# A four-layer gated transformer: layer 0's attention, norms and routing run as a pipeline over groups of 512 tokens, with reciprocals from ScalarE's Ln and Exp and a Newton step

## The chip, the cores and the metric

The kernel runs on one core of a Trainium2 chip. The metric is the device time of one execution in microseconds. A core has five engines with queues of their own, each of which works its instructions off in order: TensorE (PE: matmuls, with a second row for its weight loads), VectorE (DVE), ScalarE (ACT), GpSimd (POOL) and SyncE (SP, which here only issues DMAs). ACT and POOL issue DMAs too. Every wait between engines is a semaphore.

## The reference, cut to what matters

There are four layers; each adds a gated cross-attention and a gated mixture of experts to the residual x of 2 x 1024 tokens of 256 values. The change is in layer 0 alone:

```python
x = x + tanh(g_xattn[0]) * L0_xattn(layernorm(x), ctx, Wq, bq, ..., Wo, bo, gamma, beta)
x = x + tanh(g_ffn[0])   * L0_ffn(layernorm(x), Wr, br, W1, b1, W2, b2)
```

As the kernel computes it, layer 0's attention is linear. With h = layernorm(x), q = elu(h Wq + bq) + 1 and k the same of the context; kv = k^T v and ksum = the sum of k over the context's 64 tokens, per batch. The attention's values are (q kv) / (q ksum + 1e-6), with the division element by element per channel; these go through Wo, plus bo, plus h; a layer norm with gamma and beta follows, and the result times the gate is added to x.

Layer 0's experts: h = layernorm(x), softmax over 8 experts of h Wr + br, each token goes to its best expert. Tokens are sorted by expert into tiles of 128 slots (at most 23 tiles); each tile goes through that expert's W1, ReLU, W2, and is added back into x with its weight.

All values are float32.

## The kernel before, in words

The 2048 tokens lie in SBUF as `xs`, 16 tiles of 128 tokens by 256 values; four tiles are a group of 512 tokens. The kernel's stages follow one another: `xattn0` (layer 0's attention), `moe0` (its experts), `middle` (layer 1 and layer 2's attention), `moe_capacity` for layer 2, `heads_xattn` (layer 3's attention), `moe_capacity` for layer 3. A scheduler lays the instructions of each engine in an order when the program is built, from the order in the source and from estimated costs; instructions of neighbouring stages are mixed where the data allow. Tiles come from pools with a fixed number of buffers; a tile waits until the buffer's last reader is through.

`xattn0` in the order of its source:

- Four loads of weights, then k, v, kv and ksum of the context (L236, L239), copied out of PSUM by `evac`, which takes DVE and ACT in turn (L147, L145).
- `normed` (all four groups first): `norm_group` calls `stats` (bn_stats L154 and bn_aggr L155 per tile; then 1/sqrt by an integer first guess, L160 and L161, and three Newton rounds of three DVE instructions on four columns, L165 to L168), writes h with one DVE instruction per tile (L178), transposes it on PE (L186) and copies the transposes to hT, one half by DVE, one by ACT.
- For each group and each of the two halves of the channels (128 channels by 512 tokens; the prediction calls this a chunk): hT times Wq on PE; DVE takes min(.+bq, 0) into `qlo` (L258), ACT its Exp (L259) and the Relu of the positive part (L261), POOL adds both into q (L262); DVE computes the denominator `rden` (L263) and its reciprocal (L267). Then q times kv on PE and the product with `rden` on DVE (L272, `att`).
- For each tile: att times Wo on PE, plus bo on DVE (L277), plus h on POOL (L278), then `stats` again, two DVE instructions for the normed value and gamma (L282, L286), and two POOL additions into xs, of beta and of y (L287, L288).

`moe0` then takes the norms of all four groups again, stores h and x in two DRAM tables `hd` and `xd` (SP, L719), and calls `route`: router logits of all 16 tiles into one PSUM tile, softmax and choice by small DVE steps on 128x128 values (L628 to L650), ranks by cumulative matmuls with `upper` and `ones` (L661, L663). Sixteen more matmuls give the counts per expert (L813, `cnt`). From the counts come the expert of each of the 23 tiles (`ex_i`, `wrow`, L820 to L853) and each token's slot; `invert` turns the slots into a table of token indices by one-hot matmuls (`ohl`, `ohh`, L691 to L704; `idx`, L710). Only then does the loop over the 23 tiles run: POOL gathers W1, W2 and the biases by `wrow` (L858, into the six buffers of `wpool`) and the tokens by `idx` (L739), PE computes, POOL scatters the result into `xd` (L772).

## Time and profile before

| What | Value |
|---|---|
| runs shown | 2466.1, 2443.22, 2464.13 us; median 2464.13 us |
| profiled execution, its own time | 2454.52 us |
| its span in the trace | 2452.7 us, mean granted PE clock 0.922 |
| PE busy | 2199.9 us (90% of the span) |
| DVE busy | 1255.2 us (51%) |
| ACT busy | 757.9 us (31%) |
| POOL busy | 1072.5 us (44%) |
| DMA | 235.07 MB, mean 96 GB/s |

How to read the profile: a group's row gives line, engine, operation, output<-inputs, shapes and count, then busy us and mean ns of one, then the idle time of the engine just before and who ended it. A timeline row gives start and duration in us, engine, line, operation, and in brackets the idle time before it. A row of a stretch gives for each engine the busy us and in brackets the number of instructions, then PE's granted clock (1.00 is full), the DMA share and GB/s. L12 is line 12 of the kernel.

### The profile page before, as it was taken

The numbers are of one execution on the slowest core, as the hardware profiler recorded it, in microseconds if no ns is written. First come the engines' busy times: TensorE is split into PE (matmuls) and PEld (weight loads), VectorE is DVE, ScalarE is ACT, GpSimd is POOL, SyncE is SP. The second block draws the span as 40 slices with busy tenths as digits, with TensorE's granted clock in tenths as the row PEclk, the third lists the DMA queues.
The fourth block names the chain that finished last, engine by engine and source line by source line (L and its number), as shares of the span: only waits on it lengthen the run. The fifth ranks groups of instructions, "written<-read, shape, count | busy, mean of one in ns | idle before, by whom it ended". The sixth has DMA issues, their size and how long they took to land.

```text
span 2452.7 us, 27852 instructions
## 1 busy us (share of the span) xinstructions
PE 2199.9 (90%) x10132; PEld 1787.2 (73%) x10132; DVE 1255.2 (51%) x2742; ACT 757.9 (31%) x1431; POOL 1072.5 (44%) x1229
## 2 busy tenths in 40 slices
PE   5558887899999999999999999999968996986997
PEld 3357775588888778887788887888856774565775
DVE  7851003676566765655865656566551116663111
ACT  1003332353333533334433334333311221330221
POOL 3316664236666346665366664666303320000331
PEclk9758998899999989999999999999958998875998
DMA  3018887012222123222132222222413543010442
GB/s 97 26 59 270 275 248 241 1 52 86 86 86 87 50 63 91 89 88 73 48 95 88 88 91 78 86 86 86 141 66 86 139 112 92 18 58 22 116 116 51
DMA packets 97544, 235.07 MB, mean 96 GB/s; under 512 B 13184, under 2 KB 41088, under 8 KB 86976
## 3 DMA queue, kind: packets, MB, share of 16 engines
q1 hardware_dynamic: 70880, 159.14, 20.3%
q0 software_dynamic: 21456, 68.92, 10.3%
q10 hardware_dynamic: 5072, 5.23, 0.6%
q8 instruction: 81, 1.33, 0.2%
q14 instruction: 55, 0.45, 0.1%
HBM read 211.10 MB, written 24.25 MB: 96 GB/s over the span
## 4 chain that ended last, share of the span: by engine, by line
PE 74%; DVE 11%; DMA 5%; POOL 3%; issue 2%; ACT 2%; POOLq 0%; ACTq 0%; DVEq 0%; SPq 0%
PE ps_b L1036 12%; PE ps_m L198 10%; PE ps_e L1036 8%; PE ps_a L1036 8%; PE ps_y L765 8%; PE ps_b L1081 6%; PE ps_a L1081 4%; PE ps_e L1081 4%; PE ps_y L198 3%; PE ps_y L434 2%; DMA xg<-hd,idx 2%; PE ps_m L704 1%; PE ps_tr L186 1%; DMA xd_L<-y_ff,idx 1%; PE ps_y L386 1%
## 5 line engine op out<-in xcount | busy, mean ns | idle before, releaser
L1036 PE MATMUL ps_b<-xsum,w 128*128 128x256 f32 x1536 | 388.2, 381 | 2.3 <-DVE c L1062 2.2
L1036 PEld LDWEIGHTS ps_b<-xsum,w 128*128 128x128 f32 x1536 | 289.7, 190 | 47.6 <-issue 4.6
L943 POOL TENSOR_TENSOR w<-w 128x256 f32<-128x256 f32 x192 | 140.8, 734 | 404.0 <-DMA w<-in_L_Wu_dram 174.6
L1036 PE MATMUL ps_a<-hT,w 128*128 128x256 f32 x1024 | 270.0, 384 | 0.7 <-DVE hT L147 0.6
L198 PE MATMUL ps_m<-xT,w 128*128 128x128 f32 (+2 forms) x1248 | 253.8, 364 | 11.8 <-DVE xT L147 11.7
L765 PE MATMUL ps_y<-w,mid 128*128 128x256 f32 (+1 forms) x1136 | 252.8, 379 | 0.0
L198 PEld LDWEIGHTS ps_m<-xT,w 128*128 128x128 f32 x1248 | 188.5, 200 | 71.9 <-DVE xT L147 19.3
L765 PEld LDWEIGHTS ps_y<-w,mid 128*128 128x128 f32 (+1 forms) x1136 | 206.6, 184 | 38.9 <-issue 2.7
L988 ACT COPY u<-ps_b 128x512 f32<-128x512 f32 (+1 forms) x192 | 98.9, 515 | 411.0 <-PE ps_b L1081 264.0
L1036 PEld LDWEIGHTS ps_a<-hT,w 128*128 128x128 f32 x1024 | 194.2, 193 | 31.2 <-issue 3.2
L772 POOL DMA_INDIRECT xd_L<-y_ff,idx x48 | 74.9, 1561 | 232.4 <-DVE y_ff L771 135.8
L770 DVE TENSOR_TENSOR y_ff<-ps_y,b 128x256 f32<-128x256 f32 (+1 forms) x48 | 20.3, 423 | 298.0 <-PE ps_y L765 298.0
L944 POOL TENSOR_TENSOR w<-w 128x256 f32<-128x256 f32 x192 | 166.9, 869 | 0.0
L946 POOL TENSOR_TENSOR w<-w 128x256 f32<-128x256 f32 x192 | 158.9, 827 | 14.7
L945 POOL TENSOR_TENSOR w<-w 128x256 f32<-128x256 f32 x192 | 164.8, 859 | 0.0
L1036 PE MATMUL ps_e<-xsum,w 128*128 128x256 f32 x512 | 134.4, 383 | 0.0
L1036 PE MATMUL ps_e<-hT,w 128*128 128x256 f32 x512 | 134.1, 382 | 0.0
L1081 PE MATMUL ps_b<-t,w 128*128 128x256 f32 x512 | 132.8, 384 | 0.0
L1081 PE MATMUL ps_a<-b,w 128*128 128x256 f32 x512 | 132.0, 379 | 0.0
L970 ACT COPY ps_b<-ps_a 128x512 f32<-128x512 f32 (+1 forms) x192 | 96.5, 502 | 109.5 <-DVE b L1066 63.5
L1098 POOL TENSOR_TENSOR m<-m,accT 128x256 f32<-128x256 f32 x60 | 71.7, 1195 | 124.1 <-ACT m L976 110.4
L145 ACT COPY xT<-ps_tr 128x128 f32<-128x128 f32 (+2 forms) x39 | 13.4, 344 | 355.7 <-PE ps_tr L748 289.4
(306 smaller groups left out, 3928.5 us busy)
## 6 DMA issues: line engine op xcount, KB each, us to landing
w<-in_L_Wg_dram SPq DMA_DIRECT2D x64, 512.0 KB, 4.1
w<-in_L_Wu_dram SPq DMA_DIRECT2D x64, 512.0 KB, 4.1
w<-in_L_Wd_dram SPq DMA_DIRECT2D x64, 512.0 KB, 3.7
w<-in_L_W_dram SPq DMA_DIRECT2D x32, 1024.0 KB, 4.9
xd_L<-xs SPq DMA_DIRECT2D x8, 512.0 KB, 2.9
hd_L<-h SPq DMA_DIRECT2D x8, 512.0 KB, 3.0
xs<-in_x_dram SPq DMA_DIRECT2D x4, 512.0 KB, 10.5
xd<-xs SPq DMA_DIRECT2D x4, 512.0 KB, 2.9
```

The costliest lines, as they stand in the source:

```text
L198: T.matmul(ps, lhsT=lhs(c), rhs=rhs(c), start=(c == 0), stop=(c == n - 1))
L765: T.matmul(ps[:w, :], lhsT=mid[:, f, at : at + w], rhs=w2[:, f, :], start=(f == 0), stop=(f == NF - 1),)
L772: G.indirect_dma_start(out=xd[:, :], out_offset=bass.IndirectOffsetOnAxis(ap=idx[:w, j0 + s : j0 + s + 1], axis=0), in_=y[:w, :], in_offse ...
L943: G.tensor_add(s[0], a21, a22)
L944: G.tensor_sub(s[1], s[0], a11)
L945: G.tensor_sub(s[2], a11, a21)
L946: G.tensor_sub(s[3], a12, s[1])
L970: A.copy(self.b, self.pa)
L988: A.copy(u2, self.b)
L1036: T.matmul(ps[:, q * 256 : (q + 1) * 256], lhsT=lhs[kind][:, q, :], rhs=xr[kind], start=(first and q == 0), stop=True, skip_group_check=True,)
L1081: T.matmul(ps, lhsT=wd[kind][:, q, :], rhs=m["rhs"][kind][:, q * 256 : (q + 1) * 256], start=(clear and q == 0), stop=True, skip_group_che ...
L1098: G.tensor_add(sb, sb, acc[:, i, j])
```

## The change

`xattn0` and the routing of `moe0` become one pipeline over the four groups, with three parts: `begin` (norm, q, the first guess of the reciprocal), `finish` (kv, Wo, second norm, addition into xs) and `onward` (the experts' norm and routing of this group). In the source order begin runs one group ahead of finish and two ahead of onward. The routing works per group (`choose`), with a running count `before` (`cnt`) carried from group to group.

The reciprocal 1/d becomes a guess r = Exp(-Ln(d)) on ACT and one Newton step, r (2 - d r). The sign is turned: DVE computes att = (d r - 2) * (ps * r), the product with Wo then has the wrong sign, and it is subtracted from h + bo. 1/sqrt in these norms becomes Exp(-0.5 Ln(v)) on ACT and one Newton round. An explicit load puts the table with both Ln and Exp on ACT after the gates' Tanh. h and both hT copies of these norms are made by ACT. h + bo and x + beta are made once per group by POOL, on 128x1024 values.

```diff
-    A.activation(gates, gates, AF.Tanh)
+    tanh = A.activation(gates, gates, AF.Tanh)
+    with tc.issue_after(tanh.ins):
+        A.preload_act_table_set("natural_log_exp_and_others")
...
+        if by_log:                                   # in stats
+            y = small.tile([P, TG], F32, name="y0")
+            A.activation(y, ve, AF.Ln)
+            A.activation(y, y, AF.Exp, scale=-0.5)
...
-        for i in range(3):
+        for i in range(1 if by_log else 3):
...
+            off = small.tile([P, TG], F32, name="off")   # in norm_group
+            V.scalar_tensor_tensor(off, mv[:, :, 0], -1.0, rstd, ALU.mult, ALU.mult)
...
+                A.activation(
+                    h[:, t, :], xg[:, t, :], AF.Identity,
+                    bias=off[:, t : t + 1], scale=rstd[:, t : t + 1],
+                )
...
-            evac(c, hT[:, c, :], ps)
+            evac(1 if by_act else c, hT[:, c, :], ps)
...
+            def begin(g):
+                h, hT = norm_group(g, pt, hpool, hTp, by_act=True)
+                w = wpool.tile([P, 2048], F32, name="w")
+                q, inv = (w[:, i : i + 1024].rearrange("p (c n) -> p c n", c=NC) for i in (0, 1024))
...
                     V.tensor_scalar(lo, ps, bq, 0.0, ALU.add, ALU.min)
                     A.activation(lo, lo, AF.Exp)
-                    hi = two.tile([P, GW], F32, name="qhi")
-                    A.activation(hi, ps, AF.Relu, bias=bq)
-                    G.tensor_add(q[:, c, :], lo, hi)
-                    V.tensor_scalar(
-                        rden[:, c, :], q[:, c, :], ksum[:, b, c : c + 1], 1e-6,
-                        ALU.mult, ALU.add,
-                    )
-                    V.reciprocal(rden[:, c, :], rden[:, c, :])
+                    A.activation(q[:, c, :], ps, AF.Relu, bias=bq)
+                    G.tensor_add(q[:, c, :], q[:, c, :], lo)
+                    ks = ksum[:, b, c : c + 1]
+                    A.activation(inv[:, c, :], q[:, c, :], AF.Ln, bias=tiny, scale=ks)
+                    A.activation(inv[:, c, :], inv[:, c, :], AF.Exp, scale=-1.0)
+                    den = two.tile([P, GW], F32, name="den", bufs=6)
+                    A.activation(den, q[:, c, :], AF.Identity, bias=tiny, scale=ks)
+                    V.tensor_mul(den, den, inv[:, c, :])
+                    dens.append(den)
+                G.tensor_add(h, h, rows[:, R_BO0, :].unsqueeze(1).to_broadcast([P, TG, D]))
+                xg = residual(g)
+                G.tensor_add(xg, xg, bet.unsqueeze(1).to_broadcast([P, TG, D]))
...
+            def finish(g):
...
-                    V.tensor_mul(att[:, c, :], ps, rden[:, c, :])
+                    V.tensor_mul(att[:, c, :], ps, inv[:, c, :])
+                    V.scalar_tensor_tensor(
+                        att[:, c, :], dens[c], 2.0, att[:, c, :], ALU.subtract, ALU.mult
+                    )
...
-                    V.tensor_add(y[:, t, :], ps, rows[:, R_BO0, :])
-                    G.tensor_add(y[:, t, :], y[:, t, :], hs[g][:, t, :])
-                mv, rstd = stats(y, TG)
+                    V.tensor_sub(y[:, t, :], h[:, t, :], ps)
+                mv, rstd = stats(y, TG, True)
...
-                    V.tensor_mul(y[:, t, :], y[:, t, :], gam)
-                    G.tensor_add(xt, xt, bet)
-                    G.tensor_add(xt, xt, y[:, t, :])
+                    V.scalar_tensor_tensor(
+                        y[:, t, :], y[:, t, :], mv[:, t, 0:1], gam, ALU.subtract, ALU.mult
+                    )
+                    V.scalar_tensor_tensor(
+                        xt, y[:, t, :], rstd[:, t : t + 1], xt, ALU.mult, ALU.add
+                    )
+            def onward(g):
+                h, hT = norm_group(g, pt, hp2, by_act=True)
+                routed(g, h, hT, pr)
+            begun = {}
+            begin(0)
+            for i in range(NG + 2):
+                if i + 1 < NG:
+                    begin(i + 1)
+                if 0 <= i - 1 < NG:
+                    finish(i - 1)
+                if 0 <= i - 2:
+                    onward(i - 2)
...
+    def choose(psp, rp, g, hT, which, bias, top, before):    # as route, for one group
...
+        T.matmul(ps[:, :W], lhsT=upper, rhs=flat, start=True, stop=False)
+        for k in range(1, TG):
+            T.matmul(
+                ps[:, k * E : W], lhsT=ones, rhs=flat[:, : (TG - k) * E],
+                start=False, stop=(k == TG - 1),
+            )
+        pc = psp.tile([P, 512], F32, name="ps_m")
+        for t in range(TG):
+            T.matmul(
+                pc[:, :E], lhsT=ones, rhs=both[:, t, :], start=(t == 0), stop=(t == TG - 1)
+            )
...
+        V.tensor_add(before, before, pc[:, :E])
...
+            def routed(g, h, hT, psp):
+                ts = slice(g * TG, (g + 1) * TG)
+                for d, src in ((hd, h), (xd, residual(g))):
+                    nc.sync.dma_start(
+                        d[g * GW : (g + 1) * GW, :].rearrange("(t p) d -> p t d", p=P), src
+                    )
+                ((p1, o, _, rk),) = choose(psp, rp, g, hT, 0, e_bias[:, 0, :], 1, cnt)
...
+                V.tensor_tensor(
+                    ohl[:, ts], ramp.unsqueeze(1).to_broadcast([P, TG, P]), bc(lo, P),
+                    ALU.is_equal,
+                )
```

The low half of a token's slot, its one-hot `ohl` and its number are thus made per group; after the last group `moe0` adds the tile of its expert, makes `ohh` in two halves of 8 tiles and runs the same 16 matmuls to `idx`. The tile loop is unchanged in the source. In the built order of the changed kernel the order of the tile loop on POOL differs at its start (two weight gathers ahead of the first gather of tokens, where it was three), and the instruction lists of the engines agree from the end of layer 0's experts on.

## The prediction

> **What bounds the kernel now.** I read the page first, then a table of stretches, the groups of VectorE (DVE) instructions, and last the timeline around the hand-over to the experts.
>
> ```profile
> span 2452.7 us, 27852 instructions
> ...
> PE   5558887899999999999999999999968996986997
> DVE  7851003676566765655865656566551116663111
> ```
>
> A slice is 61 us. TensorE (PE) is full from slice 8 on; the change touches the first three slices only. So what counts is the time at which the experts of layer 0 can start.
>
> ```profile
> 30.00:40.00 10.00, 7.49 (x15) 2.99 (x14) 10.00 (x24) 3.00 (x5) 2.84 (x4) 0.83 0.00 0
> 100.00:110.00 10.00, 2.11 (x3) 1.08 (x4) 9.65 (x21) 1.21 (x2) 3.54 (x4) 0.50 0.15 52
> 140.00:160.00 20.00, 17.37 (x78) 16.07 (x78) 8.20 (x35) 1.76 (x3) 0.00 (x0) 0.50 0.24 79
> 160.00:180.00 20.00, 10.72 (x64) 10.62 (x64) 9.15 (x36) 0.31 (x1) 3.16 (x2) 0.59 0.03 7
> 240.00:260.00 20.00, 17.26 (x110) 15.03 (x109) 1.96 (x6) 6.82 (x19) 14.27 (x14) 1.00 0.89 279
> ```
>
> Columns: stretch, length, then PE, weight load, DVE, ScalarE (ACT), GpSimd (POOL) busy, PE clock, DMA share, GB/s. From 30 to 135 us DVE is the bound (10.00 and 9.65 of 10). From 135 to 178 us nothing is: layer norm, router and ranks are one chain of short steps, with PE at half clock. From 178 us on the experts pull weights at a DMA share near 0.9.
>
> ```profile
> L267 DVE RECIPROCAL rden<-rden 128x512 f32<-128x512 f32 x8 | 26.7, 3340 | 0.0
> L178 DVE TENSOR_SCALAR h<-xs,mv,rstd 128x256 f32<-128x256 f32 x28 | 12.7, 514 | 0.0
> L282 DVE TENSOR_SCALAR y_sb<-y_sb,mv,rstd 128x256 f32<-128x256 f32 x16 | 9.0, 606 | 0.0
> L263 DVE TENSOR_SCALAR rden<-q_sb,ksum 128x512 f32<-128x512 f32 x8 | 4.3, 531 | 0.0
> ```
>
> Eight reciprocals of 3.34 us take a quarter of DVE's 105 us.
>
> ```profile
> 33.60 1.26 POOL L262 TENSOR_TENSOR q_sb<-qlo,qhi 128x512 f32<-128x512 f32 x1
> 33.65 1.24 DVE L161 TENSOR_SCALAR yi<-yi 128x4 int32<-128x4 int32 x1
> ...
> 173.78 0.17 DVE L818 COPY cnt<-ps_m 128x8 f32<-128x8 f32 x1 [4.60 <-PE ps_m L813]
> ...
> 176.55 0.19 DVE L853 CAST wrow<-ex 128x23 int32<-128x23 f32 x1
> ...
> 178.03 2.68 POOL L858 DMA_INDIRECT w<-in_L_W_dram,wrow  x1 [0.30 <-DVE ohh L695]
> ...
> 188.41 0.24 DVE L710 TENSOR_SCALAR idx<-ps_m,spare 128x23 int32<-128x23 f32 x1 [7.16 <-PE ps_m L704]
> ```
>
> wrow at 176.7 us opens the weight stream, idx at 188.7 the gather of tokens; the first expert matmul comes at 192.9. I count the gain in wrow.
>
> **The reciprocals.** DVE loses 26.7 + 4.3 us and gains, per chunk (one group, one half of the channels), den times inv and (den - 2) times att: two 128x512 passes of about 0.60 (nearest row: att L272, 0.68 out of PSUM), 9.6 in all. ACT gains Ln, Identity and Exp per chunk, 24 passes. Rows: Exp L259 0.63, Relu with a bias column L261 0.67; so some 0.65, 15.6 us. **A rule against it**: the Trainium skill, "ScalarE: Activation LUTs", What it computes, says to leave reciprocals to VectorE; What ACT_TABLE_LOAD costs prices an ACTIVATE at 186 ns + 0.833 ns an element + 93 ns per column operand. Ln and Identity have two such columns, 0.80 us each by the page, Exp 0.61: 17.7 us. The rows show only 0.04 us for one column, so I take 15.6; the page's 2 us more would be on the path only in part. DVE is the bound and ACT idles, so by the rows the rule fails here: 31.0 off DVE against 9.6 back. A table load costs 1.28 in the trace (gates); the change adds one, in the wait for the gates at the start, free; if Ln and Exp switched tables the price would be up to 16 x 1.28 = 20 us, but the built instruction list holds only the one load between gates and the middle.
>
> **The norms.** h (L178) and both hT copies go to ACT (32 x about 0.45, 8 x 0.59), two of three Newton rounds and the yi steps go (about 20 us of the DVE groups L160 to L168, most of it port waits), L282 and L286 (9.0 + 6.0) become two fused 128x256 passes (32 x 0.41 = 13). DVE's busy time falls by some 50 us, ACT's rises by 40. Neither is the gain, since the order of the queues decides.
>
> **The longer POOL adds.** xs + bet and h + bo become eight 128x1024 adds: between 2.35 us (line through 0.77 for 256 and 1.30 for 512 columns) and 3.0 (four times 0.75); I take 2.7. The two lines from 33.6 us show a DVE instruction of four columns held for the whole POOL add: 1.24 us. The Trainium skill, "SBUF — State Buffer", Who interferes with whom, says the same of every DVE instruction with two SBUF inputs against a GpSimd one that reads SBUF: the later one waits for all of it. So the wait per meeting rises from 1.3 to 2.7 us. By the row alone (tensor_scalar) the norm of group 2 would meet none, and start 3 us sooner; by the rule, its q and rstd steps meet xs + bet and h + bo. I count 3 us there.
>
> **The path, from the built order.**
> 1. First qlo at 30.2 us before, about 28 after (the first 20 us are input DMA, both hT copies are on ACT, the 3 us lock is in it); then ACT still has the rest of group 2's h: Exp at 29.7.
> 2. Groups 0 to 2 are six chunks. Each next Exp of lo stands on ACT behind this chunk's last Exp: 0.54 (Exp, start to start in the trace) + 0.67 + POOL add 1.30 + Ln 0.70 + 2 x 0.55 = 4.3. Queued behind the Ln that waits for POOL are the two passes and hT copies, and PE waits for those. 6 x 4.3 = 26, and 2 more for POOL's xs + bet of group 2 in front: 57.
> 3. Group 3's statistics stand in DVE's queue behind y of group 0, whose rest stands behind the last den product of group 2. From there to rstd of group 3 are some 22 instructions, 8 us: 65. h, transposes, hT, wq: 5. Two chunks at 4.3, and POOL's two 2.7 us adds in front, 1.5: 80.
> 4. From den(3,1) to rstd of onward(2) DVE has 174 instructions: 12 y subtractions, 24 fused passes at 0.34 (start to start), 28 statistics pairs at 0.40, seven 128x512 at 0.60, 74 small of routing, rstd and copies at about 0.08 and two ohl of 0.6: 4.1 + 8.2 + 11.1 + 4.2 + 6.1 + 1.2 = 35. Waits for wo (before: 1.0, 1.06 and 1.31 us in three groups), for the router and Ln/Exp: between 2 and 18 (PE at full clock, or at half); I take 6, as before's clock was 0.8 to 0.9 where PE had this much to do. 121.
> 5. Tail, two groups in turn: h, transposes, hT, router at half clock 7.5 + 0.7 (before: 8.5); routing of 128x32 steps at 0.2: 3; cumulative matmuls 16 x 0.165 = 2.6; router of group 3 3.6; routing 3; 2.6; ranks and cnt 0.8; then cmp to wrow, before 2.8, now 5.6, because ohl and six ohh passes stand ahead of wrow: 29. **wrow 150, against 176.7: 27 us sooner.**
>
> The long count over 16 tiles (62 records, 4.92 + 5.35) leaves the path; the four short ones, 16 records each, lie beside other work except in the tail. ohl off the path saves 2 us of the 11.9 from wrow to idx, and ohh ahead of wrow 2 more; idx comes 7 us after wrow. POOL now issues two weight loads before the gather instead of three; 2 MB need about 8 us at 270 GB/s, as long as that wait, so nothing is lost. If DMA sets the experts' pace the end moves by 27, if the token loop does by 31: **29**. On SP the stores of xd and hd are now interleaved per group (hd(g) behind xd(g+1)); the last hd is stored in the tail's 29 us, 3 us long: hidden.
>
> The profiled execution took 2454.5 us (span 2452.7): 2454.5 - 29 = 2425.5. Its own time lies between the runs shown (2443 to 2466, median 2464); against that median the result would read 1.6% lower, against itself 1.2%.
>
> **Rivals.**
> - *The bubbles close* (0.22). If DVE worked without a wait from 29 us on, its queue is 24 + 35 us and wrow comes at 29 + 59 + 29 = 117: 60 sooner. For: DVE has had no idle time in the stage. Against: step 2 makes it wait for ACT and POOL. Half of the bubbles filled: 45 us, **2410**.
> - *PE at half clock sets the pace* (0.20). In step 4 a group has 16 wo records at 0.43, 8 transposes 1.95, router 3.6: 12.4 us of PE at half clock against 11.7 of DVE, in turn for each tile; waits become 18 instead of 6: gain 17, **2438**. For: clock 0.50 from 100 us. Against: PE idles less than before.
> - *The port lock* (0.08). POOL's adds sum to 8 x 2.7 + 8 x 1.3 = 32 us, all before 80 us, where DVE has some 28 instructions with two SBUF inputs. If each POOL add holds such a one that others wait for, up to 32 us come on top of the path: 29 - 32 = -3, **2458**. It decides from 29 us of such waits. Against: ACT paces that stage, and DVE has slack there.
>
> The forecast has 0.50, with its own range of a gain of 18 to 38 us. With run noise of about 10 us the range is 2402 to 2450: it takes in the closed bubbles at 45 and the half clock. One per cent, 24.6 us, is about what a measurement of this kernel can tell from no change: faster 0.36 (of the forecast) + 0.22 = 0.58; same 0.14 + 0.20 + 0.02 = 0.36; slower 0.06.
>
> **What would show it.** The weight gathers start near 150 us; the ACT timeline shows 4.3 us a chunk up to 57 us; DVE idles 20 us or more between 30 and 80 and hardly after 80; POOL adds of 2.4 to 3 us with DVE instructions of that length beside them; the expert stage keeps 9.4 us a tile. Wrong: if wrow comes before 135 or after 165, or if it comes at 150 and the kernel's end does not move with it.

## The result and the profile after

The changed kernel took 2439.65 us (median of 20 runs, 2431.99 to 2454.38) beside 2459.43 us for the kernel before (20 runs). The ratio over all these runs is 0.9943, 95% interval 0.9929 to 0.9957; it is not the quotient of the two medians, which lie 19.8 us apart. Of 2459.43 us it makes 14.0 us, between 10.6 and 17.5, where the forecast was 29. In the profiled executions the spans are 2452.7 and 2435.4 us. A gain under 1% was the "same" of the prediction, to which it gave 0.36.

The page of the changed kernel, its span and the busy tenths of TensorE (PE) and VectorE (DVE) in slices of 61 us:

```profile
span 2435.4 us, 27851 instructions
...
PE   5668887899999999999999999999968996886997
DVE  5631113675565766655855656566551116663111
```

DVE's first two digits were 7 and 8; they are 5 and 6. PE's row is full from slice 8 on, as before. So work did leave DVE, and the question is what the end gained from it. The same five stretches as before (length, then PE, weight load, DVE, ScalarE (ACT), GpSimd (POOL) busy, PE clock, DMA share, GB/s):

```profile
30.00:40.00 10.00, 8.44 (x21) 4.59 (x22) 1.76 (x4) 6.60 (x13) 6.67 (x4) 0.69 0.00 1
100.00:110.00 10.00, 6.02 (x37) 4.89 (x35) 8.30 (x41) 2.45 (x7) 0.00 (x0) 0.84 0.15 52
140.00:160.00 20.00, 14.84 (x65) 13.65 (x64) 7.13 (x42) 2.07 (x6) 0.00 (x0) 0.50 0.08 27
160.00:180.00 20.00, 11.00 (x51) 10.45 (x52) 5.70 (x30) 1.28 (x4) 10.21 (x11) 0.51 0.57 210
240.00:260.00 20.00, 17.12 (x101) 15.01 (x100) 2.04 (x6) 6.42 (x18) 12.77 (x13) 0.91 0.83 252
```

In the first row DVE fell from 10.00 busy of 10 to 1.76, and no other engine is full either: ACT 6.60, POOL 6.67, PE 8.44 at a clock of 0.69. A bound was taken away and a chain of hand-overs stands in its place. In the last row, the expert stage, PE's clock is 0.91 (1.00 before) and the weights come at 252 GB/s (279).

From 28 us to wrow, the index list that opens the weights' stream, the first row below is the kernel before, the second the changed one:

```profile
28.00:176.60 148.60, 93.53 (x310) 61.91 (x308) 116.65 (x333) 14.47 (x25) 42.10 (x52) 0.70 0.08 29
28.00:165.00 137.00, 90.84 (x319) 61.22 (x320) 79.19 (x319) 50.14 (x102) 22.58 (x14) 0.72 0.09 31
```

DVE lost 37.5 us of work and gained 25.9 us of idle time (148.60 - 116.65 = 32.0; 137.00 - 79.19 = 57.8). The stretch became 11.6 us shorter: what is left of 37.5 when 25.9 are waited away. The groups of DVE instructions of that stretch name the waits (busy us, mean ns, then the idle time ahead and who ended it):

```profile
L281 DVE TENSOR_SCALAR qlo<-ps_m,cols 128x512 f32<-128x512 f32 x8 | 6.0, 749 | 16.9 <-PE ps_m L217 16.9
L292 DVE TENSOR_TENSOR den<-den,w 128x512 f32<-128x512 f32 x8 | 5.6, 698 | 7.5 <-ACT w L289 7.5
...
L727 DVE TENSOR_TENSOR r_cum<-ps_m,cnt 128x32 f32<-128x32 f32 x4 | 0.8, 192 | 5.7 <-PE ps_m L717 5.7
L684 DVE TENSOR_TENSOR r_pr<-ps_m,e_bias 128x32 f32<-128x32 f32 x4 | 0.8, 192 | 9.9 <-PE ps_m L217 9.9
```

The largest, 16.9 us, is for the first product of a group (qlo). The timeline shows what it waits for:

```profile
26.01 2.27 DVE L176 SCALAR_TENSOR_TENSOR q<-q,ve 128x4 f32<-128x4 f32 x1
...
30.95 0.61 ACT L282 ACTIVATE qlo<-qlo 128x512 f32<-128x512 f32 x1
31.12 2.35 POOL L297 TENSOR_TENSOR xs<-xs,bet 128x1024 f32<-128x1024 f32 x1 [2.86 <-ACT h L192]
...
34.72 0.81 ACT L288 ACTIVATE w<-w,tiny,ksum 128x512 f32<-128x512 f32 x1 [0.96 <-POOL w L284]
...
36.67 0.61 ACT L282 ACTIVATE qlo<-qlo 128x512 f32<-128x512 f32 x1
...
69.34 0.16 DVE L189 SCALAR_TENSOR_TENSOR off<-mv,rstd 128x4 f32<-128x4 f32 x1
69.53 2.08 ACT L192 ACTIVATE h<-xs,off,rstd 128x256 f32<-128x256 f32 x4 [0.82 <-DVE off L189]
72.81 5.85 PE L217 MATMUL ps_m<-hT,wq 128*128 128x512 f32 x8 [0.46 <-ACT hT L150]
76.70 0.75 DVE L281 TENSOR_SCALAR qlo<-ps_m,cols 128x512 f32<-128x512 f32 x1 [7.21 <-PE ps_m L217]
...
164.98 0.18 DVE L1029 CAST wrow<-ex 128x23 int32<-128x23 f32 x1
```

From 69.34 to 76.70 us DVE, ACT and PE hand one group's norm, transposes and first product to each other, each idle while another works, and DVE stands 7.21 us. wrow comes at 165.0 instead of 176.6.

The other half of the result lies in the expert stage. The last of its 23 scatter-adds, in the kernel before and in the changed one:

```profile
407.87 1.58 POOL L772 DMA_INDIRECT xd<-y_ff,idx  x1 [7.67 <-DVE w L340]
```

```profile
404.03 1.58 POOL L899 DMA_INDIRECT xd<-y_ff,idx  x1 [7.78 <-DVE w L392]
```

Of the 11.6 us only 3.8 are left here. From the first scatter to the last a tile took 9.25 us before (204.4 to 407.9, 22 steps) and 9.88 after (186.6 to 404.0). So two things are to be explained: 11.6 us at wrow instead of 27, and 7.8 us lost behind it.

The spans of the two profiles differ by 17.3 us, though, and only 3.8 of these had been gained at the last scatter. The rest lies behind it, where both kernels run the same instructions (stretch and columns as above, the kernel before first):

```profile
407.87:2452.70 2044.83, 1902.07 (x8594) 1547.10 (x8592) 1092.73 (x2233) 666.54 (x1194) 876.33 (x1017) 0.94 0.27 81
404.03:2435.40 2031.37, 1889.25 (x8594) 1537.84 (x8592) 1090.33 (x2233) 665.25 (x1194) 876.92 (x1017) 0.94 0.27 82
```

The same 8594 matmul records kept PE busy 12.8 us longer in the kernel before; with one digit more its clock is 0.936 there and 0.944 in the changed kernel. In the profiles of the 18 other kernels of this document this part took 2023.3 to 2045.4 us, 2034.5 on average, and less time the higher the clock (0.950 with 2023.3 us, 0.937 with 2045.4). So the causes are read from the times up to the last scatter, and the end gives the size only.

### The profile page after: what moved, and what is told of

Read it like the earlier page. It is cut to its first block, busy times and chain, and to the rows that moved or that the text cites. A ratio compares the mean times of both kernels' runs of the same rounds, so it can differ in the third digit from the quotient of the medians.

```text
span 2435.4 us, 27851 instructions
## 1 busy us (share of the span) xinstructions
PE 2189.6 (90%) x10132; PEld 1782.7 (73%) x10132; DVE 1210.5 (50%) x2695; ACT 797.9 (33%) x1523; POOL 1054.2 (43%) x1189
## 3 DMA queue, kind: packets, MB, share of 16 engines
q0 software_dynamic: 21456, 68.92, 10.3%
## 4 chain that ended last, share of the span: by engine, by line
PE 76%; DVE 10%; DMA 4%; POOL 2%; ACT 2%; issue 2%; POOLq 0%; DVEq 0%; ACTq 0%; SPq 0%
PE ps_b L1210 13%; PE ps_m L217 11%; PE ps_e L1210 9%; PE ps_a L1210 9%; PE ps_y L892 8%; PE ps_b L1255 6%; PE ps_a L1255 4%; PE ps_e L1255 4%; PE ps_y L486 2%; PE ps_y L217 2%; DMA xg<-hd,idx 1%; DVE st L159 1%; PE ps_tr L205 1%; DMA xd_L<-y_ff,idx 1%; PE ps_y L438 1%
## 5 line engine op out<-in xcount | busy, mean ns | idle before, releaser
L217 PE MATMUL ps_m<-xT,w 128*128 128x128 f32 (+2 forms) x1248 | 260.6, 372 | 16.4 <-DVE xT L152 16.0
L217 PEld LDWEIGHTS ps_m<-xT,w 128*128 128x128 f32 x1248 | 195.6, 208 | 76.1 <-DVE xT L152 23.2
```

What stands on the lines that cost most here:

```text
L217: T.matmul(ps, lhsT=lhs(c), rhs=rhs(c), start=(c == 0), stop=(c == n - 1))
```

## The experiments

The times at which the milestones came, each in the one profiled execution, and the measured ratios. "To last" is the time from wrow to the last scatter; "order" is that of POOL's queue in the expert stage (a: as in the changed kernel, b: as in the kernel before, t: token rows ahead). Each ratio is taken against runs of the kernel before in the same round (medians from 2451 to 2457 us for e1 to e17), so it is not the quotient with 2459.43.

| Kernel | order | wrow | last scatter | to last | median us | ratio to before, 95% |
|---|---|---|---|---|---|---|
| before | b | 176.6 | 407.9 | 231.3 | 2459.43 | 1 |
| changed | a | 165.0 | 404.0 | 239.1 | 2439.65 | 0.9943 (0.9929 to 0.9957) |
| e1 scatter late | own | 166.4 | 404.0 | 237.7 | 2441.68 | 0.9940 (0.9917 to 0.9962) |
| e2 idle matmuls | a | 164.7 | 404.3 | 239.6 | 2443.18 | 0.9941 (0.9919 to 0.9964) |
| e3 tokens ahead | t | 165.3 | 400.0 | 234.7 | 2441.51 | 0.9941 (0.9919 to 0.9962) |
| e4 before, tokens ahead | t | 174.5 | 415.4 | 240.9 | 2458.41 | 1.0010 (0.9994 to 1.0025) |
| e5 e3 + Relu on DVE | t | 166.0 | 379.0 | 213.1 | 2417.74 | 0.9864 (0.9840 to 0.9887) |
| e6 half the weights | a, smaller loads | 165.4 | 399.6 | 234.2 | 2433.93 | 0.9937 (0.9913 to 0.9960) |
| e7 pipeline alone | a | 173.9 | 405.7 | 231.8 | 2444.18 | 0.9968 (0.9955 to 0.9981) |
| e8 reciprocals alone | b | 156.9 | 390.5 | 233.6 | 2424.51 | 0.9883 (0.9855 to 0.9910) |
| e9 changed, order b | b | 166.5 | 397.2 | 230.6 | 2435.07 | 0.9922 (0.9890 to 0.9954) |
| e10 norms on DVE | a | 177.4 | 415.4 | 238.0 | 2452.79 | 0.9996 (0.9972 to 1.0019) |
| e11 den on DVE | a | 165.9 | 404.7 | 238.8 | 2437.95 | 0.9936 (0.9918 to 0.9955) |
| e12 e8 + t + Relu on DVE | t | 155.7 | 390.4 | 234.8 | 2427.93 | 0.9889 (0.9853 to 0.9924) |
| e13 attention's pipeline only | b | 163.5 | 399.1 | 235.5 | 2433.27 | 0.9917 (0.9889 to 0.9945) |
| e14 heads early | a | 154.2 | 390.8 | 236.6 | 2431.16 | 0.9904 (0.9881 to 0.9928) |
| e15 e8, order a | a | 152.5 | 397.6 | 245.2 | 2435.30 | 0.9917 (0.9888 to 0.9946) |
| e16 e14, order b | b | 154.2 | 385.6 | 231.5 | 2423.69 | 0.9884 (0.9856 to 0.9912) |
| e17 e14 + t + Relu on DVE | t | 154.1 | 365.6 | 211.6 | 2403.43 | 0.9805 (0.9774 to 0.9837) |

How far a single profile carries can be read off kernels that have the same instructions in the same order up to wrow. Seven with the front of the changed kernel (it, e1, e2, e3, e5, e6, e9) have wrow at 164.7 to 166.5 us, three with that of e8 (it, e12, e15) at 156.9, 155.7 and 152.5, the kernel before and e4 at 176.6 and 174.5, and e14, e16 and e17 at 154.1 to 154.2. A difference of 2 us, between the three 4.4, is no finding.

### First guesses at the expert stage: e1 to e4

In POOL's queue of the changed kernel the scatter of two tiles before stands between a tile's two weight gathers; in the kernel before it stood behind both for the first 14 tiles. So the two orders differ in their middle too, and not at the start alone. With w for a weight gather, 1 and 2 for the bias gathers, g for the token gather and S for the scatter, e1 changes every later tile:

```
-  w S w 1 2 g
+  w w S 1 2 g
```

> The changed kernel with one thing moved: in every expert tile the scatter of two tiles before stands behind both weight gathers in GpSimd's queue (the order of the first 14 tiles of the kernel before) instead of between them, so that one gather less (1.25 us) stands between a scatter and the next token gather. In the changed kernel the 22 steps from the first scatter (186.6 us) to the last (404.0) took 9.88 us each, with 10 of 22 tiles at a granted clock of 0.80 to 0.85. Theory Q, the queue's order lengthens the ring scatter, token gather, transposes, products, scatter: steps of about 9.3 us, last scatter near 391, the kernel 10 to 13 us faster than the changed one (some 2427 beside 2440). Theory C, the half clock of every second tile costs the time and is no matter of the order: steps stay near 9.9, under 4 us of difference. Theory D, the weights' transfer rate sets the step (DMA busy 0.80): no difference.

Last scatter 404.0 as in the changed kernel, 0.9940: the scatter's place between the weight gathers, taken alone, is not the cause. Theory Q falls in this form.

e2 fills PE's gaps:

```
  ffn(..., held)
+ fill = pm.tile([P, 512], F32, name="ps_m")
+ for i in range(6):
+     T.matmul(fill[:, :P], lhsT=ident, rhs=xT[:, i % NC, :P], start=(i == 0), stop=(i == 5))
```

> The changed kernel with six idle matmuls of 128x128 (about 0.24 us each at full clock, 1.4 us a tile, results unread) queued on TensorE behind each expert tile's second product, in the gap of about 2.1 us in which it waits for the next token rows; GpSimd's order is the changed kernel's. Theory C: the gap closes, nearly all 22 tiles show a granted clock of 1.00, the 1.7 us that each of some 10 slowed tiles lost come back: steps of 9.2 to 9.5 us, last scatter 10 to 16 us earlier than 404.0. Theory Q: the clock may rise but GpSimd's ring keeps its pace: steps of 9.6 to 10, within 4 us of the changed kernel. Theory D: no difference. If the idle matmuls come to stand in front of rows that have landed: up to 1 us a tile slower.

The suspicion came from four tiles of the changed kernel, each row from one tile's transposes to the next (length, PE busy, PE clock, DMA share, GB/s):

```profile
311.56:321.95 10.39, 7.68 (x51) 1.00 0.76 235
321.95:332.09 10.14, 9.46 (x51) 0.83 0.89 286
332.09:342.24 10.15, 7.67 (x51) 1.00 0.79 218
342.24:352.12 9.88, 9.46 (x50) 0.83 0.87 285
```

Every second one of them has a clock of 0.83 and 1.8 us more of PE. With the idle matmuls:

```profile
311.22:320.41 9.19, 8.85 (x64) 1.00 0.87 258
320.41:331.88 11.47, 9.39 (x65) 1.00 0.87 288
331.88:341.07 9.19, 8.85 (x65) 1.00 0.73 191
341.07:350.93 9.86, 9.01 (x64) 1.00 0.84 270
```

The clock is 1.00 in all of them, and in 21 of the stage's 22 steps; the steps are no shorter (9.92 us on average, last scatter 404.3). The idle matmuls are work of their own, so PE is as busy as at the low clock; but in e6 below tiles with a clock of 1.00 and no such matmuls take 9.8 to 9.9 us as well. Theory C falls.

e3 gathers each tile's token rows one tile earlier, e4 gives the same loop to the kernel before:

```
-  tile j:  ... 1(j) 2(j) g(j)
+  tile j:  ... 1(j) 2(j) g(j+1)
```

> The changed kernel with the token gather of each expert tile put into GpSimd's queue one tile earlier (two ahead for the first tile), and the scatter behind both weight gathers. The ring then spans three tiles. Theory Q: the step falls to what GpSimd's own six issues take, 0.95 us each and 1.62 for the scatter with 0.30 between, 8.4 us a tile; last scatter near 186.6 + 22 x 8.45 = 372, the kernel some 30 us faster than the changed one (about 2409), TensorE's clock at 1.00 since 7.7 of 8.4 us are busy. Theory C alone: the clock recovers only if the gaps close, so between 0 and 16 us. Theory D: transfers busy 0.80 of 9.88 us leave 7.9 us as the least, but if the landing time of 6.7 us of the weights sets the step, then 9.3 to 9.9 as now.

> The kernel before with the same expert loop as the token-ahead version of the changed kernel (same order in GpSimd's queue). Theory Q: steps of 8.4 to 8.5 us here as well, last scatter near 204.4 + 22 x 8.45 = 390 instead of 407.9, about 17 us faster than the kernel before; with equal loops the changed kernel's lead at the first scatter (17.9 us) stands undiminished at the last: the two token-ahead versions end 16 to 20 us apart. Theory D: no gain, and the lead at the last scatter shrinks to some 4 us as between the two kernels themselves.

Neither ended faster than the kernel whose loop it changes. The tiles of e3 alternated between 8.2 and 11 to 12 us. In the long ones ACT's eight Relu passes came 1.44 us apart instead of 0.44, and PE waited for them. Theory D, traffic, was left, and the next pair bears on it.

### What the expert stage does not hang on: e5, e6

e5 takes e3 and puts the Relu passes on DVE:

```
- A.activation(mid[:, f, :n], ps[:, :n], func, bias=b1[:, f : f + 1])
+ V.tensor_scalar(mid[:, f, :n], ps[:, :n], b1[:, f : f + 1], 0.0, ALU.add, ALU.max)
```

> The token-ahead version of the changed kernel with the eight bias-and-Relu passes of every expert tile (128x128 each) on VectorE instead of ScalarE. In the token-ahead version tiles alternated between 8.2 and 11.2 to 12.1 us; in the long ones ScalarE took its eight passes 1.44 us apart (0.44 in the short ones) though TensorE had issued their products, and TensorE stood waiting for a free PSUM buffer; no weight load was late. Theory S, ScalarE's own dispatch stalls: on VectorE all tiles take 8.2 to 8.6 us, last scatter 370 to 380, about 2410 to 2418. Theory D, the weights' traffic sets the pace and the stall only shows where the slack is: tiles still average 9.6 to 9.9 us, last scatter 398 to 406, the stall now seen on VectorE. Theory E, the product itself is late (TensorE's records show issues, not ends): the passes on VectorE are 1.44 us apart as well.

8.60 us a tile, last scatter 379.0, 0.9864. Theory S seemed right; e12 took that back (below). e6 leaves W2 out of the changed kernel's loop and multiplies by W1 in its place, so that half of the weights are loaded (its output is not the reference's):

```
- w2 = view2(rows_of(wpool.tile([P, 2048], F32, name="w"), "L0_W2", wrow, j))
+ rows_of(two.tile([P, NF], F32, name="b1x"), "L0_b1", wrow, j)
+ w2 = w1.rearrange("p c (f d) -> p (c f) d", d=D)
```

> The changed kernel, its order in GpSimd's queue kept, with the second weight gather (1 MB) of every expert tile replaced by a small one (128 rows of 32 bytes), and the first weight read in its place: the products have the same shapes, the output is not the reference's in the expert stage, and half of the weights' traffic is gone. Theory D (traffic sets the tile's 9.9 us): 7.9 us of transfers a tile fall to about 4.5, tiles take GpSimd's 8.4 us or the ring's 9.2 at most, no stall of ScalarE, last scatter 372 to 390. Theories S and Q: the stall and the alternation stay, 9.6 to 9.9 us a tile, last scatter near 400.

```profile
280.56:290.46 9.90, 7.73 (x51) 1.00 0.54 147
290.46:300.28 9.82, 7.73 (x50) 1.00 0.56 149
300.28:310.13 9.85, 7.73 (x50) 1.00 0.56 147
```

At 147 GB/s instead of 252 these tiles still take 9.8 to 9.9 us (9.69 on average over the stage), and none of its Relu passes is late. So it is not the weights' traffic that sets the pace: theory D falls. Of the theories named, the order in which things stand in the queues is left, more of it than the one scatter of e1.

### The front, split in two: e7, e8

e7 keeps the pipeline and puts DVE's reciprocals back; e8 gives the kernel before the new reciprocals and nothing else.

```
e7:
- A.activation(inv, q, AF.Ln, bias=tiny, scale=ks); A.activation(inv, inv, AF.Exp, scale=-1.0)
- A.activation(den, q, AF.Identity, ...); V.tensor_mul(den, den, inv)   and the (den - 2) pass
+ V.tensor_scalar(inv, q, ks, 1e-6, ALU.mult, ALU.add); V.reciprocal(inv, inv)
e8: the same lines the other way round, in the kernel before
```

> The changed kernel with the reciprocals of attention done by VectorE's reciprocal as in the kernel before (eight of 3.26 us, and one multiply-add of 0.45 to 0.7 each), the four ScalarE and VectorE passes of the guess and the Newton step gone; the pipeline over groups stays. ScalarE's part of a chunk falls from about 3.5 us to 1.3. If ScalarE's longer chunk is what made the start late (first step that failed): the eight reciprocals put 26 us on VectorE, which has some 10 us idle between 28 and 88 us, less 8 products of 0.65 and 8 of 0.7: the routing indices (wrow) at 165 + 10 to 18 = 175 to 183, that is the pipeline alone gains nothing there. If VectorE's slack hides them: wrow within 4 us of 165.

> The kernel before with only the reciprocals changed: ScalarE's logarithm and exponential as first guess, the Newton step folded into the products, no pipeline over groups and the normalizations as before. VectorE loses eight reciprocals of 3.26 us and eight multiply-adds and gains sixteen passes of about 0.68: 26 + 4 - 11 = 19 us less of the 82 us that it was busy in attention. If VectorE bounds that stage: wrow near 176.6 - 15 to 19 = 158 to 162, earlier than in the changed kernel. If the passes on ScalarE (eight chunks of 2.2 us more) and their waits take the place: 168 to 176. At the end of the experts, by theory D, under half of either is left.

The stretch of e8 from 28 us to wrow, beside the two above:

```profile
28.00:156.90 128.90, 87.50 (x314) 60.92 (x312) 96.48 (x331) 30.08 (x49) 41.84 (x50) 0.76 0.10 33
```

This is the widest finding. wrow comes 2.6 us earlier with the pipeline alone (two runs of the old front are 2.1 apart), 19.6 with the reciprocals alone, and 11.6 with both. e8's 19.6 are the 20.2 us that left DVE in its stretch (116.65 to 96.48 us busy, idle time unchanged at 32 us), one for one, and its last scatter is 17.4 us earlier. The pipeline takes 8 us of that away again (by the spread of wrow given above, 8 to 14), although it removes another 17 us of DVE's work.

### The order in the expert stage: e9, e15

e9 is the changed kernel with POOL's queue set as in the kernel before, e15 is e8 with that of the changed kernel:

```
before:   2ww1wgw12gww1g2Sww12Sgww1S2g  9 x wwS12g  9 x wSw12g  SS
changed:  2ww1g ww12g                   3 x wwS12g 18 x wSw12g  SS
```

> The changed kernel with GpSimd's queue of the expert stage (and with it VectorE's order there) set instruction for instruction as in the kernel before: three weight gathers ahead of the first token gather, scatters behind the later token gathers at first, then behind both weight gathers, and between them from the 14th tile on. Theory L, the order is what made the changed kernel's tiles slower (238.9 us from wrow to the last scatter, 231.3 before, 233.6 with the reciprocals alone): 231 to 234 us from wrow, last scatter 396 to 399, no stalled ScalarE passes, the kernel 5 to 8 us faster than the changed one (about 2433 beside 2440). Theory R, the stall comes and goes between executions (the pipeline alone had the changed kernel's order and no stall, 231.8 us): median within 3 us of the changed kernel's, whatever the profile shows.

> The kernel before with the changed reciprocals alone, and GpSimd's queue of the expert stage in the changed kernel's order. Theory L, that order costs 5 to 8 us whatever stands in front of it: 238 to 241 us from wrow (157) to the last scatter (233.6 in its own order), last scatter 395 to 398, ratio to the kernel before 0.990 to 0.992 (0.988 in its own order). Theory R, the stall comes and goes: 231 to 235 us, ratio 0.987 to 0.989.

The last scatters of e9, and then of e15:

```profile
397.15 1.58 POOL L903 DMA_INDIRECT xd<-y_ff,idx  x1 [11.67 <-DVE w L392]
```

```profile
397.64 1.58 POOL L787 DMA_INDIRECT xd<-y_ff,idx  x1 [13.57 <-DVE w L351]
```

e9 wins 6.9 us against the changed kernel, e15 loses 7.1 against e8 (counted from wrow 8.5 and 11.6), and the ratios go the same way (0.9943 to 0.9922, 0.9883 to 0.9917), though in each pair the intervals overlap. A third pair follows below: e14 and e16, 5.2 us. Over all profiles with a tile's work unchanged (without e2 and e6), the five with order b took 230.6 to 235.5 us from wrow to the last scatter, mean 232.5; the six with order a took 231.8 to 245.2, mean 238.2, and only e7 of them lies among the first. Theory L holds, by 5 to 12 us in single profiles. Counted from wrow, the seventh scatter came after 77.5 us in e9 and 77.4 in the changed kernel, and the last sixteen steps took 153.1 and 161.6: there the start is not where the two part. In e15 both stretches are longer than in e8 (84.3 and 160.9 us, 77.6 and 156.0). Which feature of the order does it was not tried apart. One trace of a way is that late Relu passes (counted below) go with order a and a long stage: e7, with order a and none of them, lost nothing. That they are the way is not shown.

### What the pipeline costs: e10, e11, e13, e14

Two shifts between ACT and DVE:

```
e10: - A.activation(h[:, t, :], xg[:, t, :], AF.Identity, bias=off, scale=rstd)
     + V.tensor_scalar(h[:, t, :], xg[:, t, :], mv, rstd, ALU.subtract, ALU.mult)
     - evac(1 if by_act else c, hT[:, c, :], ps)
     + evac(c, hT[:, c, :], ps)
e11: - A.activation(den, q[:, c, :], AF.Identity, bias=tiny, scale=ks)
     + V.tensor_scalar(den, q[:, c, :], ks, 1e-6, ALU.mult, ALU.add)
```

> The changed kernel with the eight group normalizations back on VectorE (32 passes of 128x256) and every second copy of the transposed rows too; ScalarE keeps the first guess of rstd, the reciprocals and the Newton step stay as changed. Theory A, ScalarE's chain (two copies of 0.5 after four passes of 0.5 a group, then 3.5 us a chunk) paces the pipeline, VectorE being idle 58 of the 137 us from 28 us to wrow: wrow 4 to 8 us earlier, 157 to 161. Theory V, VectorE's own queue paces it: 32 passes of 0.41 to 0.52 less the 8 small ones, and 8 copies of 0.68, some 18 us more on VectorE: wrow 5 to 15 us later, 170 to 180. Theory P, TensorE and the round trips pace it: within 3 us of 165.

> The changed kernel with one ScalarE pass of every chunk (Identity with two column operands, 0.80 us, the denominator that the Newton step multiplies) made by VectorE instead (0.45 to 0.7 us); eight chunks. Theory A: a chunk on ScalarE falls from 3.6 to 2.8 us, six of them lie on the path to the third group's start and two more behind it: wrow 4 to 6 us earlier, 159 to 161. Theory V: 8 passes of 0.5 more on VectorE: 2 to 4 us later. Theory P: within 2 us of 165.

e10's wrow is 12.4 us later, so for the norms moving them to ACT was right. e11 takes a pass of 0.80 us off each chunk on ACT, and wrow moves by 0.9 us, the wrong way and within the spread: the price of one ACT pass is not what paces the start. The next two change the order of the work. e13 takes the routing out of the pipeline, e14 writes each group's head (norm, transposes, copies) one group earlier, with a fourth buffer for the normed rows that this needs:

```
e13: xattn0 without onward(); then normed(...) and route(...) of all 16 tiles as before
e14:   head(0); head(1); begin(0)
       for i in range(NG + 2):
     +     if i + 2 < NG: head(i + 2)
           if i + 1 < NG: begin(i + 1)
```

> The changed kernel with attention's pipeline and reciprocals kept, but normalization and routing of the expert layer as in the kernel before: after attention, all four groups normalized, routed in one batch of 16 token tiles. GpSimd's order in the expert stage comes out as in the kernel before. Theory T, routing group by group is what costs (26 small VectorE instructions four times at 0.16 to 0.19 us, 18 us instead of 7.5, and 15.6 us of waits for the router's and the counting products): wrow at 150 to 157, not later than with the reciprocals alone (156.9). Theory H, the head of each group comes late whatever follows: wrow 162 to 172. In either case 231 to 234 us from wrow to the last scatter.

> The changed kernel with normalization, transposes and copies of group g+2 written ahead of the chunks of group g+1, so that a group's first product no longer waits for its head; one more buffer for the normalized rows. Theory H: of the 16.9 us in which VectorE waits for the first products about half goes, wrow 157 to 160, 5 to 8 us earlier than the changed kernel's 165.0. Theory T: the wait turns up later, at the router's products; wrow within 3 us of 165.

e13: wrow 163.5. Routing in pieces costs no more than routing in one batch, theory T falls. e14: wrow 154.2, 10.8 us earlier, with the same work on DVE and ACT (79.7 and 49.7 us busy); e16 and e17 repeat it. The waits of the two groups of e14, the same ones as above:

```profile
L281 DVE TENSOR_SCALAR qlo<-ps_m,cols 128x512 f32<-128x512 f32 x8 | 6.0, 746 | 8.3 <-PE ps_m L217 5.7 <-POOL w L284 2.6
...
L292 DVE TENSOR_TENSOR den<-den,w 128x512 f32<-128x512 f32 x8 | 5.5, 685 | 2.9 <-ACT w L289 2.9
```

16.9 + 7.5 us became 8.3 + 2.9: 13.2 us of waits gone for 10.8 us at wrow. Theory H holds, for the place and the buffer together. The kernel before made all four heads ahead of the first chunk; the pipeline had put each of them into the chain.

### The sum, and how far it goes: e16, e12, e17

e16 has both mends: heads early, and order b in POOL's queue.

> The changed kernel with both mends: each group's head one group earlier, and GpSimd's queue of the expert stage in the order of the kernel before. If the causes are the two named and add: wrow 154, 231 to 234 us to the last scatter, that at 385 to 388 (404.0 in the changed kernel, 390.8 with the heads alone, 397.2 with the order alone), 27 to 31 us faster than the kernel before: ratio 0.987 to 0.989, about what the prediction named. If the weights' stream limits the earlier start: last scatter 390 to 393, ratio 0.990 as with the heads alone.

```profile
385.61 1.58 POOL L912 DMA_INDIRECT xd<-y_ff,idx  x1 [7.02 <-DVE w L401]
```

Last scatter 385.6, ratio 0.9884: against 2454.2 us of the kernel before beside it that is 28.5 us. Against the changed kernel's ratio the heads alone bring 9.6 us (0.9904), the order alone 5.2 (0.9922), both together 14.5. They add, as far as intervals of 6 us can tell.

At the last scatter e16 is 22.3 us ahead of the kernel before; the other 6 lie behind it. And e8, the reciprocals without any pipeline, has the same ratio, 0.9883. At wrow the two are within the spread (154.1, and 152.5 to 156.9), and at the last scatter e16 is 4.9 us earlier. So even with both mends no gain of the pipeline over the reciprocals alone is shown at the end.

e12 is e8 with e5's loop, e17 is e14 with e5's loop.

> The kernel before with the changed reciprocals alone (no pipeline), and the expert loop with token rows gathered one tile ahead, scatters behind both weight gathers, and the Relu passes on VectorE. From parts: wrow 157, then 213 us to the last scatter as with the same loop in the changed kernel: 370, 9 us earlier than there (379.0). If the gains add: 9 us faster than that version (ratio to the kernel before 0.986): about 0.982 to 0.983, some 2408. If the weights' stream limits the earlier start (wrow to last scatter 220 or more): 0.985 to 0.987.

> The changed kernel with each group's head one group earlier and the expert loop with token rows gathered a tile ahead, scatters behind both weight gathers, and Relu passes on VectorE. By the same loop in the changed kernel (213 us from wrow to the last scatter): 154 + 213 = 367, some 9 us faster than there, ratio 0.982 to 0.984. By the same loop behind the reciprocals alone (234.7 us, products late in every second tile): 389, ratio 0.988 to 0.990. The second is taken as likelier where the tiles alternate.

e12 got no more than e8 (last scatter 390.4), e17 got what the sum of the parts named: last scatter 365.6, 8.6 us a tile, 2403.4 us, ratio 0.9805. It is the fastest version here, 2% (1.6 to 2.3) below the kernel before. Two runs of the same loop at 8.6 and one at 9.4 us a tile take back the reading of e5. In e12, with the Relu passes on DVE, they are late as well:

```profile
267.65 0.35 DVE L775 TENSOR_SCALAR mid<-ps_m,b1j 128x128 f32<-128x128 f32 x1 [0.54 <-PE ps_m L203]
268.28 0.35 DVE L775 TENSOR_SCALAR mid<-ps_m,b1j 128x128 f32<-128x128 f32 x1 [0.27 <-PE ps_m L203]
269.72 0.35 DVE L775 TENSOR_SCALAR mid<-ps_m,b1j 128x128 f32<-128x128 f32 x1 [1.09 <-PE ps_m L203]
```

PE had issued these products from 266.90 us on, six in 2.94 us. 1.44 us from pass to pass, on either engine: the delay is not ScalarE's (theory S of e5), but comes with the product or its signal (theory E, in e12 only). Pauses of 0.8 to 3 us between one Relu pass and the next (190 to 400 us) numbered 21 in the changed kernel, 23 in e1, 49 in e3, 51 in e4, 28 in e12, 3 to 10 in e2, e9, e10, e11, e14 and e15, and none in the kernel before, e5, e6, e7, e8, e13, e16 and e17. What brings them about stays open.

## Why the prediction went wrong, step by step

**The frame was right.** DVE was the bound from 30 to 135 us, and the gain at wrow decides what the experts can gain: e8, e14 and e16 carry 17 to 22 us of their 20 to 22 us at wrow to the last scatter. The loads were right in the main: over the whole kernel DVE's busy time fell by 44.7 us (some 50 said), ACT's rose by 40.0 (40 said). The gain at the end, ratio times the time before, is 4 to 13 us more than that at the last scatter in all 18 kernels that were set against the kernel before, also in those that differ from it in the loop alone (e4) or in the reciprocals alone (e8). What all 18 share is the kernel before on the other side, whose part behind the last scatter took 10.3 us more in its profile than theirs on average, with the same instructions. So this surplus is no step of the prediction, and 10.2 of the 14.0 us measured here are of that kind. Whether the kernel before has the lower clock there as a rule or had it in this profile is not shown.

**Step 1** held: first qlo at 28.66 us (28), with the port lock where it was put (q held 2.27 us by a POOL add of 2.34). The Exp behind it came at 30.95 (29.7).

**Step 2, the chunks: 4 us late.** den(2,1) came at 61.1 us, 57 said; 1.2 of that is the late Exp of step 1. Undisturbed, a chunk took 4.5 us on ACT from Exp to Exp (42.90 to 47.41, 77.49 to 82.02), 4.3 said. Most of the rest is the second chunk, 6.2 us (36.67 to 42.90), in which a long POOL add, h + bo, stood in front of q and ACT waited 2.14 us for it:

```profile
36.90 2.79 POOL L295 TENSOR_TENSOR h<-h,rows 128x1024 f32<-128x1024 f32 x1 [2.21 <-PE ps_tr L205]
```

The prediction had put xs + bet there and not this one. The price of a pass was too low as well, but little hangs on it, as e11 shows: Ln took 0.81 and Identity 0.80 us, where 0.65 had been taken from the rows of one column operand and the Trainium skill ("ScalarE: Activation LUTs", What ACT_TABLE_LOAD costs) gives 0.80 for two; Exp took 0.61. The page was right, the nearest row was not. The page's advice to use VectorE's reciprocal (What it computes) has another reason than time, accuracy issues of ScalarE's own Reciprocal function. The change does not use that function, so the advice was no rule against it, and e8 (0.9883, 0.9855 to 0.9910, DVE 20.2 us less busy) does not contradict it.

**Step 3, the head of group 3: 2.4 us short.** 8 us from den(2,1) to rstd was right (8.2), h to qlo took 7.4 instead of 5: the eight wq records took 5.85 us, at a clock of 0.50 from 69.3 to 76.7 us, behind a wait of PE of 9.6. The prediction had this head in its path and priced it nearly right, but did not ask what it meant: each group's head, which the kernel before made ahead of all chunks, now lay in series with them. e14 shows that this place costs 10.8 us; it is what the pipeline could have gained, and only 2.4 of it are an error of the sum.

**Step 4, the waits: the largest miss before wrow, 7 us.** From den(3,1) to rstd of onward(2):

```profile
86.65:134.45 47.80, 30.18 (x132) 23.39 (x130) 37.90 (x174) 9.22 (x26) 0.00 (x0) 0.76 0.16 56
```

47.8 us instead of 41: DVE was busy 37.9 (35 said) and waited 9.9 (6 said). It waited for PE's products, 2.9 us for the router's, 2.9 for the counts, 2.2 for the ranks and 1.7 for wo. The 6 had been taken from a clock of 0.8 to 0.9; it was 0.76. **Step 5: 30.5 instead of 29.** Together 4.1 + 0.2 + 2.4 + 6.8 + 1.5 = 15.0 us: wrow at 165.0 instead of 150. The path was the right one; its terms were too small, the waits between the engines above all. A wrow of 165.0 lies on the prediction's own mark for wrong, 165.

**The expert stage: the step that failed outright.** "POOL now issues two weight loads before the gather instead of three; ... nothing is lost", and 9.4 us a tile. A tile took 9.88 us, and of the 11.6 us at wrow 7.8 were lost. Setting the order back brought 6.9 us (e9) and 5.2 (e16 against e14), setting it in cost 7.1 (e15). The prediction priced the bytes of one load and not the order of the 138 queue entries around it. The alternative that it kept open, that DMA sets the pace, falls by e6. By what way the order acts stays open.

**The rivals.** PE at half clock named 2438 and the result is 2439.65, but that is luck: its waits in step 4 were to be 18 us and were 9.9, and the expert stage was no part of it. The bubbles did not close; DVE's idle time grew by 25.9 us. The port lock is real and stayed on few instructions: from 19 to 88 us POOL's adds held a copy for 2.38 us, q for 1.28 and 2.27, and one att pass for 1.62 instead of 0.69.

With the two losses mended (e16) the change brings 28.5 us, where 29 had been forecast. That nearness is in part luck too: 22.3 of them stand at the last scatter, where 27 to 31 had been named, and the reciprocals alone (e8) bring 28.7.

## What to carry to other kernels

When work leaves the engine that bounds a stage, look at once at what was hidden under it: here every us taken off DVE by the reciprocals alone arrived, and the pipeline, which took off more, gave 8 us or more back in waits. So price the parts of a change apart; the simple part can be the whole gain. In a software pipeline look for the first stage (norm, transpose, first product) in series with the rest: here it had to stand one step further ahead than the source had it, and moving a few lines brought 10 us beside the 14 of the whole change. And a change in front of a stage whose queue a scheduler orders can change that order: set the two orders side by side before calling the later stage untouched.

## What the runs showed of the hardware

- Filling PE's gaps with 1.4 us of idle matmuls a tile raised the granted clock from 0.83 to 1.00 in the tiles shown and brought no time. In the changed kernel the low clock came behind a gap of only 1.32 us and 0.34 more (at 321.95 us), and not behind one of 1.39 (at 313.34); the Trainium skill ("TensorE: Matmul & The Clock Gate", HAM oscillation — how this bites in real kernels) names gaps of over some 3.4 us. The trace decides: shorter ones can go with it. What decides between two such gaps is not shown.
- Relu passes came in multiples of about 0.72 us after products that PE had issued long before, on ScalarE and on VectorE, in some kernels in every second tile and in others never. With half of the weights' traffic (e6) there were none, but neither were there in e7, e8 and others with all of it; the cause is not shown.
- POOL's own issues are a floor of the expert stage as long as a tile has these six: S to S in e17 is 8.22 us, one scatter of 1.62 and five gathers of 0.94 to 0.99 with 0.30 between.

```profile
271.07 1.62 POOL L917 DMA_INDIRECT xd<-y_ff,idx  x1 [0.98 <-DVE mid L900]
272.99 0.99 POOL L1065 DMA_INDIRECT b1j<-in_L_b_dram,wrow  x1 [0.30 <-issue]
274.28 0.95 POOL L1065 DMA_INDIRECT b2j<-in_L_b_dram,ex_i  x1 [0.30 <-issue]
275.54 0.95 POOL L874 DMA_INDIRECT xg<-hd,idx  x1 [0.30 <-issue]
276.79 0.94 POOL L1065 DMA_INDIRECT w<-in_L_W_dram,wrow  x1 [0.30 <-PE ps_tr L887]
278.04 0.95 POOL L1065 DMA_INDIRECT w<-in_L_W_dram,wrow  x1 [0.30 <-PE ps_m L217]
279.29 1.62 POOL L917 DMA_INDIRECT xd<-y_ff,idx  x1 [0.30 <-DVE mid L900]
```
